# A selective-scan layer's side work re-staged: dt one tile at a time through one PSUM bank, output projections through the other

## The chip, the cores and the metric

The kernel runs on one core of one Trainium2 chip. The metric is the device time of one execution in microseconds (us), taken as the median of several runs. One execution on the chip was also taken with the hardware profiler; its trace gives the start, length and releaser of every instruction. The engines are named as in the profile: PE (TensorE, matmul), DVE (VectorE), ACT (ScalarE), POOL (GpSimd) and SP (SyncE, which only issues DMAs here).

## The reference

Four layers follow one another on a tensor of 3 x 256 x 48 x 48, each with a group norm ahead and a residual behind: an attention block, a mixture-of-experts 3x3 convolution, a plain 3x3 convolution, and a selective scan (Mamba). The change touches only the last one, except that the first two chunks of it are prepared during the third layer. All of it is float32. For each batch, with L = 2304 positions, 256 channels, 512 inner channels and 16 states:

```python
x = x + L3(_gn(x))
# L3, on tokens xf of shape (B, L, 256)
xn = (xf - mean(xf)) * rsqrt(var(xf) + 1e-5) * norm_w + norm_b
x_in, z = split(xn @ in_proj_w.T)               # 512 + 512
u  = silu(causal_conv4(x_in) + conv_b)
dt_raw, B_ssm, C_ssm = split(u @ x_proj_w.T)    # 16 + 16 + 16
dt = softplus(dt_raw @ dt_proj_w.T + dt_proj_b)
def step(h, t):
    h = h * exp(dt[t][:, None] * A) + dt[t][:, None] * B_ssm[t][None, :] * u[t][:, None]
    return h, (h * C_ssm[t][None, :]).sum(-1)
y = scan(step) + u * D_param
out = (y * silu(z)) @ out_proj_w.T
```

## The kernel before

The scan layer takes the 3 x 2304 positions in 18 chunks of 384. For each chunk the 512 inner channels are four tiles (m = 0 to 3) of 128 rows, and the 16 states of a channel are worked through in two halves (h). A pair (m, h) is a **step**, so a chunk has 8 steps, and each step has 8 **scans** (parts 0 to 7), one DVE instruction of 128 x 385 each. Four scans make a **slot**; a chunk has slots 0 to 15, and step s holds slots 2s and 2s + 1.

What belongs to the scan itself runs in a fixed pattern around each step:

- ACT computes the decay factors exp(dt * A) three scans ahead (`decay`, L1758) into three PSUM slots that rotate. So the decay for scan n + 3 can only start when scan n has ended, and DVE can go on for two more scans while ACT does something else.
- DVE scans (L1766). Between steps it fills half of the next input (`fill_upper`, L1719): three units of 768 elements ahead of an even step, one ahead of an odd step. At the end of every odd step it multiplies by the gate (`gate`, L1807).
- POOL fills the other half (L1733) and multiplies the scanned states by C (`times_c`, L1783), in turn.
- PE sums the states (`add_states`, L1795 and L1800, one PSUM bank `ps_y`) and spreads rows (`spread_pe`, L1689).

Beside it, each chunk's preparation runs one and two chunks ahead and its output projection one chunk behind. These pieces are put at slots by hand: `plan`, `after` and `gating` are lists of (slot, place, relative chunk, stage). The places within a slot are MID (after its second scan), DONE (third), LATE (fourth) and PE_ (matmuls, at LATE of an even slot and at the end of the step, ahead of `add_states`, for an odd slot). `keep_order` then ties the instructions of PE, DVE, ACT and POOL to the order in which they were written down, so each engine works strictly in that order; one that waits holds up everything behind it. SP's DMA queue works in order too.

All the side matmuls share two PSUM banks, `bank[0]` and `bank[1]`. Per chunk they pass, before the change, in this order:

- slots 0 to 4: `taps` (L1264, convolution with in_proj folded in, 8 matmuls for each tile m) for the next chunk, evacuated by `take_u` (L1273);
- slots 5 to 8: `project_y` (L1353, L1355) of the chunk before, output half 0 in bank 0 and half 1 in bank 1, evacuated by `store` (L1365);
- slot 7: `silu` of u (L1278, with a table load before and one after it, L228), then `project_u` (L1284) and `take_dbc` (L1292);
- slots 8 to 12: dt in pairs of tiles: `project_dt` (L1310) into both banks, `softplus` on ACT (L1319 to L1321: Abs, then Exp and Ln over both tiles), `take_dt` on DVE (L1326, L1327), and `keep_dt`, which copies dt out on ACT (L1331) and has SP write dt and dt*u to DRAM, from where `spread` reads them back row-replicated;
- slots 12 to 15: the token norm of the chunk after next: `group_scale` (L1213), `less_mean` (L1222, both banks), `centre` (L1235, and a square into tile `sq`, L1237), `square_mean` (L1229), `inverse_root` (L1241, L1242), `normalise` on DVE (L1246);
- slots 13 to 15: `project_z` (L1341), evacuated by `take_z` (L1349).

f32 matmuls appear as two records each in the trace.

Of the kernel before, what the change touches and what calls it, by code (L numbers as in the profile page):

```python
# [83 lines left out]
def net(  # L84
# [1041 lines left out]
    def w3_rooms():  # L1126

        block = upools[0].tile([P, 6, 3, CT, 256], F32, name="u")
        block = block.rearrange("p a b c d -> p (a b c d)")
        w3v.update(divide(  # L1130
            block, ("w3sb", P, (NW3,)), ("wtap", P, (DCONV, CT, DI * P)), ("dtsb", DTR + 1, (DI * P,)),
            ("amat", P, (DI * DS,)), ("rep", P, (4, 32)), ("less", P, (2, P)), ("zero", P, (8,)),
            ("xn0", P, (CT, CH + DCONV - 1)), ("xn1", P, (CT, CH + DCONV - 1)),
        ))
        rooms["xn"] = [w3v["xn0"], w3v["xn1"]]
        pieces = [wst.tile([P, 3 * 256], F32, name="wconv") for _ in range(6)]
        halves = [t.rearrange("p (t n) -> p t n", t=2) for t in pieces]
        for name, got in zip(("xg", "sq", "ot"), (halves[:2], halves[2:3], halves[3:5])):
            rooms[name] = got
        rooms["dbc"] = [halves[5][:96, j, :] for j in range(2)]  # L1140

# [73 lines left out]
                bias=sh[:, ct : ct + 1], scale=sc[:, ct : ct + 1],  # L1215
            )

    def less_mean(k):

        for to in range(CT):  # L1220
            for ct in range(CT):
                nc.tensor.matmul(  # L1222
                    bank[to], w3v["less"][:, int(to != ct), :], k.xg[:, ct, :],
                    start=ct == 0, stop=ct == CT - 1,
                )
# [17 lines left out]

    def normalise(k):
        rs = bank[1].unsqueeze(1).broadcast_to([P, CT, CH])
        nc.vector.tensor_tensor(k.xg, k.xg, rs, ALU.mult)  # L1246

    def tokens(k):

# [54 lines left out]
        k.dt = room(k, "dt")  # L1304
        k.dtu = room(k, "dtu")

    def project_dt(k, m0):
        for j in range(2):
            m = m0 + j
            nc.tensor.matmul(  # L1310
                bank[j], w3v["dtsb"][:, m * P : (m + 1) * P], k.dbc[: DTR + 1, :],
                start=True, stop=True,
            )

    def softplus(k, m0):

        both = k.dt[:, m0 : m0 + 2, :]
        for j in range(2):
            nc.scalar.activation(k.dt[:, m0 + j, :], bank[j], AF.Abs)  # L1319
        nc.scalar.activation(both, both, AF.Exp, scale=-1.0)  # L1320
        nc.scalar.activation(both, both, AF.Ln, bias=1.0)  # L1321

    def take_dt(k, m0):
        for j in range(2):
            m, pdt = m0 + j, bank[j]
            nc.vector.scalar_tensor_tensor(pdt, pdt, 0.0, k.dt[:, m, :], ALU.max, ALU.add)  # L1326
            nc.vector.tensor_tensor(k.dtu[:, m, :], pdt, k.u[:, m, :], ALU.mult)  # L1327

    def keep_dt(k, m0):
        for j in range(2):  # L1330
            nc.scalar.copy(k.dt[:, m0 + j, :], bank[j])  # L1331
        if m0 == 0:
            k.dtd, k.dtud = {}, {}
        d = k.dtd[m0] = dram.tile([P, 2, CH], F32, name=f"dtd{m0}")
        nc.sync.dma_start(d, k.dt[:, m0 : m0 + 2, :])
        d = k.dtud[m0] = dram.tile([P // 2, 2, CH], F32, name=f"dtud{m0}")
        nc.sync.dma_start(d, k.dtu[P // 2 :, m0 : m0 + 2, :])

    def project_z(k, m, j):
        for ct in range(CT):  # L1340
# [7 lines left out]
            k.sz = room(k, "sz")  # L1348
        nc.scalar.copy(k.sz[:, m, :], bank[j])  # L1349

    def project_y(k, mo, lo=0, hi=DI):
        if lo == 0:
            nc.tensor.matmul(bank[mo], ident, k.ot[:, mo, :], start=True, stop=False)  # L1353
        for m in range(lo, hi):
            nc.tensor.matmul(  # L1355
                bank[mo], w("out", m * 256 + mo * P, P), k.sz[:, m, :],
                start=False, stop=m == DI - 1,
            )

# [66 lines left out]
    def early_preparation():  # L1428

        while (2, 1) not in stored:  # L1430
            yield
# [4 lines left out]
        while 2 not in norm3:
            yield
        group_scale(k)
        yield
# [29 lines left out]
        k = chunks[1]  # L1469
        for stage in (group_scale, less_mean, centre, square_mean, inverse_root, normalise):  # L1470
# [12 lines left out]
        take_dbc(k)  # L1483
        yield
        for m in (0, 2):
            project_dt(k, m)
            yield
            softplus(k, m)
            yield
            take_dt(k, m)  # L1490
            yield
            keep_dt(k, m)
            yield
# [483 lines left out]
```

## Time and profile before

| what | value |
|---|---|
| median of 3 runs | 3452.24 us (3449.96 to 3456.17) |
| the profiled execution, its own time | 3452.73 us |
| span in its trace (first to last instruction) | 3451.2 us |
| PE, DVE, ACT, POOL busy, whole span | 3115.5, 2937.4, 2353.3, 1430.3 us |
| scan stage of the last layer | from 2021 us (first fill by DVE) to the end |
| one chunk there (from one `project_dt` of slot 8 to the next, 2619.29 to 2697.84) | 78.55 us |

How to read it: the engines' shares of the whole span mix four layers; only the last 1430 us matter here. In that stage the trace repeats almost exactly from chunk to chunk, so one chunk can be read for all. A timeline line gives the start in us, the length in us (for a merged run, from the first start to the last end), engine, source line, operation, output <- input with shapes, how many were merged, and in brackets the idle time of that engine just before and what ended it. A waits line gives the waiting engine and its line, what it waited for, total us, how often, and the longest. A windows line gives the length of a stretch, busy us and instruction count of PE, PEld, DVE, ACT and POOL, the clock granted to TensorE as a share of full speed, the DMA share and GB/s.

### The profile page before, as it was taken

To read this page: it belongs to the slowest core of one execution; us is meant where nothing else is said; L and a number is where in the kernel's file an instruction comes from. 1 tells how busy PE (TensorE), PEld (TensorE's weight loads), DVE (VectorE), ACT (ScalarE), POOL (GpSimd) and SP (SyncE) were. 2 spreads that over 40 slices of the span, in tenths; PEclk is the share of its full clock that TensorE was granted. 3 is DMA by queue.
4 is the path that set the end of the run, shared out by engine and by line. 5 is a ranking of instruction groups with operands and counts; after the bars stand their busy time and mean duration, and the time that the engine had idled before them with its cause. 6 is when DMAs were issued, how large, how long until landed. Compare 5 with 4: busy or idle time off the path is not lost. (4 is left out here: it accounts for less than half of the span.)

```text
span 3451.2 us, 51999 instructions
## 1 busy us (share of the span) xinstructions
PE 3115.5 (90%) x20170; PEld 1496.8 (43%) x20170; DVE 2937.4 (85%) x3306; ACT 2353.3 (68%) x3508; POOL 1430.3 (41%) x385
## 2 busy tenths in 40 slices
PE   7999999999999999879999988888888888888885
PEld 4334343443433335457677753333344443333331
DVE  4799899859899994589965379999999999999998
ACT  3788888748888884422224467777777777777774
POOL 0000000000000001110000059999999999999997
PEclk9999999999999999999999998889999999988987
DMA  4000000010000003756302134444544444544441
GB/s 178 14 8 10 8 10 8 8 42 5 11 6 8 10 8 112 240 190 222 133 22 67 46 97 115 109 105 114 120 102 115 102 109 113 119 114 107 116 111 43
DMA packets 167603, 273.95 MB, mean 79 GB/s; under 512 B 30049, under 2 KB 134561, under 8 KB 165426
## 3 DMA queue, kind: packets, MB, share of 16 engines
q1 hardware_dynamic: 154114, 250.48, 26.9%
q10 hardware_dynamic: 13232, 20.06, 1.8%
q8 instruction: 160, 2.62, 0.3%
q14 instruction: 97, 0.79, 0.1%
HBM read 223.12 MB, written 47.10 MB: 78 GB/s over the span
## 5 line engine op out<-in xcount | busy, mean ns | idle before, releaser
L641 ACT ACTIVATE pt<-ps_s 128x1024 f32<-128x1024 f32 x972 | 942.4, 1022 | 154.7 <-PE ps_s L637 142.1
L1766 DVE TENSOR_TENSOR_SCAN hs<-ps_da,hs 128x385 f32<-128x385 f32 x1152 | 1003.9, 937 | 30.7 <-ACT ps_da L1758 27.3
L856 DVE TENSOR_TENSOR part<-part,pt 128x2048 f32<-128x2048 f32 x396 | 906.7, 2290 | 41.2 <-ACT pt L641 18.4
L1758 ACT ACTIVATE ps_da<-dtr,u 128x384 f32<-128x384 f32 x1152 | 656.5, 583 | 244.1 <-DVE hs L1766 225.9
L163 POOL TENSOR_TENSOR rstd<-ve,mhalf 128x2 f32<-128x2 f32 (+1 forms) x26 | 16.4, 631 | 1475.9 <-DVE ve L161 1475.9
L637 PE MATMUL ps_s<-q,kt 32*128 32x512 f32 (+1 forms) x4320 | 576.4, 592 | 0.1
L650 PE MATMUL acc<-pt,vt 128*32 128x512 f32 (+1 forms) x4320 | 520.9, 561 | 0.2
L1783 POOL TENSOR_TENSOR hc<-hs,x 128x3072 f32<-128x3072 f32 x72 | 445.6, 6188 | 18.9 <-DVE hs L1766 16.0
L1513 PE MATMUL ps_c<-vt,u 128*128 128x288 f32 x1728 | 432.7, 411 | 20.5 <-DVE u L262 20.5
L1783 POOL TENSOR_TENSOR hc<-hs,bc 128x3072 f32<-128x3072 f32 x71 | 437.8, 6166 | 17.3 <-DVE hs L1766 15.1
L1264 PE MATMUL ps_g<-u 128*128 128x384 f32 x1152 | 388.6, 492 | 7.4 <-ACT sz L1349 3.2
L1513 PEld LDWEIGHTS ps_c<-vt,u 128*128 128x128 f32 x1728 | 330.7, 192 | 117.1 <-issue 18.8
L1264 PEld LDWEIGHTS ps_g<-u 128*128 128x128 f32 x1152 | 214.8, 190 | 180.3 <-ACT ps_da L1758 19.3
L637 PEld LDWEIGHTS ps_s<-q,kt 32*128 32x128 f32 x4320 | 195.2, 183 | 199.1 <-issue 120.2
L1800 PE MATMUL ps_y<-hc,u 128*32 128x384 f32 x2304 | 245.0, 548 | 19.6 <-POOL hc L1783 19.1
L1733 POOL TENSOR_TENSOR hs<-dtur,x 128x1536 f32<-128x1536 f32 x72 | 248.9, 3457 | 6.3 <-DMA dtur<-dtud 6.3
L1733 POOL TENSOR_TENSOR hs<-dtur,bc 128x1536 f32<-128x1536 f32 x72 | 248.5, 3451 | 0.0
L650 PEld LDWEIGHTS acc<-pt,vt 128*32 128x32 f32 x4320 | 94.4, 108 | 353.4 <-issue 326.7
L1310 PE MATMUL ps_g<-wconv,u 17*128 17x384 f32 x144 | 79.2, 684 | 85.0 <-ACT x L1331 85.0
L1800 PEld LDWEIGHTS ps_y<-hc,u 128*32 128x32 f32 x2304 | 64.2, 117 | 177.8 <-issue 143.1
L1222 PE MATMUL ps_g<-wconv,u 128*128 128x384 f32 x144 | 80.3, 725 | 62.1 <-ACT x L1331 62.1
L321 POOL MEMSET xpad<- 128x212 f32 x12 | 5.7, 472 | 313.4 <-ACT xpad L1564 234.9
(246 smaller groups left out, 3624.0 us busy)
## 6 DMA issues: line engine op xcount, KB each, us to landing
wconv<-in_we SPq DMA_DIRECT2D x144, 384.0 KB, 4.2
dtr<-dtd SPq DMA_DIRECT2D x288, 192.0 KB, 3.9
dtur<-dtud SPq DMA_DIRECT2D x288, 96.0 KB, 4.2
wconv<-xd SPq DMA_DIRECT2D x36, 384.0 KB, 4.3
x<-bcd SPq DMA_DIRECT2D x72, 192.0 KB, 6.0
dtd<-x SPq DMA_DIRECT2D x36, 384.0 KB, 3.1
bc<-bcd SPq DMA_DIRECT2D x72, 192.0 KB, 6.0
yc<-ycat ACTq DMA_DIRECT2D x18, 576.0 KB, 4.7
```

Of the source, the lines that this page charges most:

```text
L637: nc.tensor.matmul(s[:, j, cols], kt[r, mt * P : (mt + 1) * P], q[r, :n], start=True, stop=True,)
L641: nc.scalar.activation(p[:, h0 : h0 + 2, :], s, AF.Exp)
L650: nc.tensor.matmul(acc[h * HD : (h + 1) * HD, :n], vt[:, mt, g * P + h * HD : g * P + (h + 1) * HD], p[:, h, cols], start=mt == 0, stop=mt ...
L856: ): nc.vector.tensor_tensor(part, first, p, ALU.add)
L1222: nc.tensor.matmul(bank[to], w3v["less"][:, int(to != ct), :], k.xg[:, ct, :], start=ct == 0, stop=ct == CT - 1,)
L1264: nc.tensor.matmul(bank[m % 2], w3v["wtap"][:, tap, ct, m * P : (m + 1) * P], k.xn[:, ct, tap : tap + CH], start=tap == 0 and ct == 0, sto ...
L1513: nc.tensor.matmul(pc[:, :HN], u[:, i, dy, ct, m * P : (m + 1) * P], vt[:, i, ct, dy * TW : dy * TW + HN], start=ct == 0 and dy == 0, stop ...
L1733: nc.gpsimd.tensor_tensor(states(s)[:, :, 2:4, 1:], chunks[at].rows[m][1].unsqueeze(1).broadcast_to([P, 2, 2, CH]), b_rows(s, 0, 2), ALU.mult,
L1758: nc.scalar.activation(slots[n % 3][:, 1 : CH + 1], chunks[at].rows[m][0][:, q, :], AF.Exp, scale=amat[:, col : col + 1],)
L1766: nc.vector.tensor_tensor_scan(b, slots[(8 * s + part) % 3][:, : CH + 1], b, 0.0, ALU.mult, ALU.add)
L1783: nc.gpsimd.tensor_tensor(hc, tiles[s][:, :, :, 1:], cb.broadcast_to([P, 2, 4, CH]), ALU.mult)
L1800: nc.tensor.matmul(k.y_ps[32 * q : 32 * q + 32, :CH], fold, hc[:, g, q, :], start=False, stop=h == 1 and g == 1,)
```

## The change

All of dt now goes tile by tile through bank 0, `project_y` and the norm go through bank 1, and a new place BEGIN (after the first scan of a slot) is used. The plan lists, which fix the order on every engine:

```diff
-    MID, DONE, LATE, PE_ = range(4)
+    BEGIN, MID, DONE, LATE, PE_ = range(5)
     plan = [
-        (12, MID, 2, group_scale),
-        (12, PE_, 2, less_mean),
-        (13, LATE, 2, centre),
+        (11, MID, 2, group_scale),
+        (11, PE_, 2, lambda k: less_mean(k, 0)),
+        (12, DONE, 2, lambda k: centre(k, 0)),
+        (12, PE_, 2, lambda k: less_mean(k, 1)),
+        (13, LATE, 2, lambda k: centre(k, 1)),
+        (13, LATE, 2, squares),
         (13, PE_, 2, square_mean),
...
         (8, LATE, 1, take_dbc),
         (8, PE_, 1, lambda k: project_dt(k, 0)),
-        (9, LATE, 1, lambda k: softplus(k, 0)),
-        (10, MID, 1, lambda k: take_dt(k, 0)),
-        (10, DONE, 1, lambda k: keep_dt(k, 0)),
-        (10, PE_, 1, lambda k: project_dt(k, 2)),
+        (9, MID, 1, lambda k: softplus(k, 0)),
+        (9, LATE, 1, lambda k: take_dt(k, 0)),
+        (10, BEGIN, 1, lambda k: keep_dt(k, 0)),
+        (10, BEGIN, 1, lambda k: project_dt(k, 1)),
+        (10, DONE, 1, lambda k: softplus(k, 1)),
+        (11, BEGIN, 1, lambda k: take_dt(k, 1)),
+        (11, MID, 1, lambda k: keep_dt(k, 1)),
+        (11, MID, 1, lambda k: project_dt(k, 2)),
         (11, LATE, 1, lambda k: softplus(k, 2)),
-        (12, MID, 1, lambda k: take_dt(k, 2)),
-        (12, DONE, 1, lambda k: keep_dt(k, 2)),
+        (12, BEGIN, 1, lambda k: take_dt(k, 2)),
+        (12, MID, 1, lambda k: keep_dt(k, 2)),
+        (12, MID, 1, lambda k: project_dt(k, 3)),
+        (12, LATE, 1, lambda k: softplus(k, 3)),
+        (13, MID, 1, lambda k: take_dt(k, 3)),
+        (13, DONE, 1, lambda k: keep_dt(k, 3)),
     ]
     after = [
...
-        (5, PE_, -1, lambda k: project_y(k, 0)),
-        (6, LATE, -1, lambda k: store(k, 0)),
-        (6, PE_, -1, lambda k: project_y(k, 1)),
-        (8, MID, -1, lambda k: store(k, 1)),
+        (8, MID, -1, lambda k: project_y(k, 0)),
+        (9, DONE, -1, lambda k: store(k, 0)),
+        (10, MID, -1, lambda k: project_y(k, 1)),
+        (11, DONE, -1, lambda k: store(k, 1)),
     ]
```

The stages themselves, cut to what differs:

```diff
-    def less_mean(k):
-        for to in range(CT):
-            for ct in range(CT):
-                nc.tensor.matmul(bank[to], w3v["less"][:, int(to != ct), :], k.xg[:, ct, :], ...)
+    def less_mean(k, to, at=1):
+        for ct in range(CT):
+            nc.tensor.matmul(bank[at], w3v["less"][:, int(to != ct), :], k.xg[:, ct, :], ...)
-    def centre(k):
-        for ct in range(CT):
-            nc.scalar.copy(k.xg[:, ct, :], bank[ct])
-        k.sq = room(k, "sq")
-        nc.scalar.activation(k.sq, k.xg, AF.Square)
+    def centre(k, to, at=1):
+        if to == 0:
+            k.xc = room(k, "xc")
+        nc.scalar.copy(k.xc[:, to, :], bank[at])
+    def squares(k):
+        nc.scalar.activation(k.xg, k.xc, AF.Square)
-    def softplus(k, m0):
-        both = k.dt[:, m0 : m0 + 2, :]
-        for j in range(2):
-            nc.scalar.activation(k.dt[:, m0 + j, :], bank[j], AF.Abs)
-        nc.scalar.activation(both, both, AF.Exp, scale=-1.0)
-        nc.scalar.activation(both, both, AF.Ln, bias=1.0)
+    def softplus(k, m, at=0):
+        t = k.dt[:, m, :]
+        nc.scalar.activation(t, bank[at], AF.Abs)
+        nc.scalar.activation(t, t, AF.Exp, scale=-1.0)
+        nc.scalar.activation(t, t, AF.Ln, bias=1.0)
-    def keep_dt(k, m0):
-        for j in range(2):
-            nc.scalar.copy(k.dt[:, m0 + j, :], bank[j])
...
-        nc.sync.dma_start(d, k.dt[:, m0 : m0 + 2, :])
...
-        nc.sync.dma_start(d, k.dtu[P // 2 :, m0 : m0 + 2, :])
+    def keep_dt(k, m, at=0):
+        nc.scalar.copy(k.dt[:, m, :], bank[at])
...
+        nc.sync.dma_start(d, k.dt[:, m, :])
...
+        nc.sync.dma_start(d, k.dtu[P // 2 :, m, :])
```

`project_dt` and `take_dt` likewise take one tile and bank 0; `project_y` and `store` take bank 1, except at the very end of the kernel, where both banks are used as before. In `spread` the tile `dtur` loses a padding: it was [128, 2, 16 + 384] of which 384 columns from the eighth on were used, and is now [128, 2, 384]. The first two chunks, which are prepared during the third layer, go through both banks as before, in the same order and with the same number of pauses.

On PE the order of one chunk from slot 5 on was `project_y` 0, `add_states`, `spread_pe`, `project_y` 1, `project_u`, `add_states`, `project_dt` 0 and 1, `add_states`. It is now `add_states`, `spread_pe`, `project_u`, `add_states`, `project_y` 0, `project_dt` 0, `add_states`, `spread_pe`, `project_dt` 1, `project_y` 1, `project_dt` 2, `less_mean` 0, `add_states`, `project_dt` 3, `less_mean` 1, `square_mean`.

More of the change, by code (lines that the diff above doesn't have):

```diff
@@ L1137, in w3_rooms @@
         halves = [t.rearrange("p (t n) -> p t n", t=2) for t in pieces]
-        for name, got in zip(("xg", "sq", "ot"), (halves[:2], halves[2:3], halves[3:5])):
+        for name, got in zip(("xg", "xc", "ot"), (halves[:2], halves[2:3], halves[3:5])):
             rooms[name] = got
@@ L1216, in group_scale @@
             )
-    def less_mean(k):
-        for to in range(CT):
-            for ct in range(CT):
[L1222 to L1225, printed above, removed]
+    def less_mean(k, to, at=1):
+        for ct in range(CT):
+            nc.tensor.matmul(
+                bank[at], w3v["less"][:, int(to != ct), :], k.xg[:, ct, :],
+                start=ct == 0, stop=ct == CT - 1,
+            )
+    def centre(k, to, at=1):
[4 more added lines that the diff above has]
+        nc.scalar.activation(k.xg, k.xc, AF.Square)
     def square_mean(k):
@@ L1229, in square_mean @@
             nc.tensor.matmul(
-                bank[1], mean2, k.sq[:, ct, :], start=ct == 0, stop=ct == CT - 1
+                bank[1], mean2, k.xg[:, ct, :], start=ct == 0, stop=ct == CT - 1
             )
-    def centre(k):
-        for ct in range(CT):
-            nc.scalar.copy(k.xg[:, ct, :], bank[ct])
-        k.sq = room(k, "sq")
-        nc.scalar.activation(k.sq, k.xg, AF.Square)
     def inverse_root(k):
@@ L1245, in normalise @@
         rs = bank[1].unsqueeze(1).broadcast_to([P, CT, CH])
-        nc.vector.tensor_tensor(k.xg, k.xg, rs, ALU.mult)
+        nc.vector.tensor_tensor(k.xg, k.xc, rs, ALU.mult)
     def tokens(k):
@@ L1305, in take_dbc, with project_dt, take_dt @@
         k.dtu = room(k, "dtu")
-    def project_dt(k, m0):
-        for j in range(2):
[L1309 to L1313, printed above, removed]
-    def softplus(k, m0):
-        both = k.dt[:, m0 : m0 + 2, :]
-        for j in range(2):
-            nc.scalar.activation(k.dt[:, m0 + j, :], bank[j], AF.Abs)
-        nc.scalar.activation(both, both, AF.Exp, scale=-1.0)
[L1321 to L1327, printed above, removed]
-    def keep_dt(k, m0):
-        for j in range(2):
-            nc.scalar.copy(k.dt[:, m0 + j, :], bank[j])
-        if m0 == 0:
+    def project_dt(k, m, at=0):
+        nc.tensor.matmul(
+            bank[at], w3v["dtsb"][:, m * P : (m + 1) * P], k.dbc[: DTR + 1, :],
+            start=True, stop=True,
+        )
+    def softplus(k, m, at=0):
[3 more added lines that the diff above has]
+        nc.scalar.activation(t, t, AF.Ln, bias=1.0)
+    def take_dt(k, m, at=0):
+        p = bank[at]
+        nc.vector.scalar_tensor_tensor(p, p, 0.0, k.dt[:, m, :], ALU.max, ALU.add)
+        nc.vector.tensor_tensor(k.dtu[:, m, :], p, k.u[:, m, :], ALU.mult)
+    def keep_dt(k, m, at=0):
+        nc.scalar.copy(k.dt[:, m, :], bank[at])
+        if m == 0:
             k.dtd, k.dtud = {}, {}
-        d = k.dtd[m0] = dram.tile([P, 2, CH], F32, name=f"dtd{m0}")
-        nc.sync.dma_start(d, k.dt[:, m0 : m0 + 2, :])
-        d = k.dtud[m0] = dram.tile([P // 2, 2, CH], F32, name=f"dtud{m0}")
-        nc.sync.dma_start(d, k.dtu[P // 2 :, m0 : m0 + 2, :])
+        d = k.dtd[m] = dram.tile([P, CH], F32, name=f"dtd{m}")
+        nc.sync.dma_start(d, k.dt[:, m, :])
+        d = k.dtud[m] = dram.tile([P // 2, CH], F32, name=f"dtud{m}")
+        nc.sync.dma_start(d, k.dtu[P // 2 :, m, :])
     def project_z(k, m, j):
@@ L1349, in take_z, with project_y @@
         nc.scalar.copy(k.sz[:, m, :], bank[j])
-    def project_y(k, mo, lo=0, hi=DI):
+    def project_y(k, mo, lo=0, hi=DI, at=1):
         if lo == 0:
-            nc.tensor.matmul(bank[mo], ident, k.ot[:, mo, :], start=True, stop=False)
+            nc.tensor.matmul(bank[at], ident, k.ot[:, mo, :], start=True, stop=False)
         for m in range(lo, hi):
             nc.tensor.matmul(
-                bank[mo], w("out", m * 256 + mo * P, P), k.sz[:, m, :],
+                bank[at], w("out", m * 256 + mo * P, P), k.sz[:, m, :],
                 start=False, stop=m == DI - 1,
@@ L1362, in residual, with store @@
         nc.sync.dma_start(k.ot, xd[k.b][:, :, k.c * CH : (k.c + 1) * CH])
-    def store(k, mo):
-        nc.scalar.copy(k.ot[:, mo, :], bank[mo])
+    def store(k, mo, at=1):
+        nc.scalar.copy(k.ot[:, mo, :], bank[at])
         nc.sync.dma_start(
@@ L1441, in early_preparation @@
             fold_taps(winx, cwb, tap)
-        less_mean(k)
+            less_mean(k, tap, tap)
         yield
-        centre(k)
+        for ct in range(CT):
+            centre(k, ct, ct)
+        squares(k)
         yield
@@ L1469, in early_preparation @@
         k = chunks[1]
-        for stage in (group_scale, less_mean, centre, square_mean, inverse_root, normalise):
+        group_scale(k)
+        yield
+        for ct in range(CT):
+            less_mean(k, ct, ct)
+        yield
+        for ct in range(CT):
+            centre(k, ct, ct)
+        squares(k)
+        yield
+        for stage in (square_mean, inverse_root, normalise):
             stage(k)
@@ L1484, in early_preparation @@
         yield
[L1485 to L1493, printed above, removed]
+        for m0 in (0, 2):
+            for stage in (project_dt, softplus, take_dt, keep_dt):
+                for j in range(2):
+                    stage(k, m0 + j, j)
+                yield
         for m in (0, 2):
@@ L1675, in spread @@
             dtr = scn.tile([P, 4, CH], F32, name="dtr")
-            dtur = scn.tile([P, 2, 16 + CH], F32, name="dtur")[:, :, 8 : 8 + CH]
+            dtur = scn.tile([P, 2, CH], F32, name="dtur")
             for t, src in ((dtr, k.dtd), (dtur, k.dtud)):
-                src = src[m & 2][:, m & 1, :]
+                src = src[m]
                 for i in range(4):
@@ L1831, in net @@
                     first_states(s + 1)
+                if part % 4 == 0:
+                    run(at, j, BEGIN)
                 if part % 4 == 1:
@@ L1856, in net @@
         for mo in range(2):
-            project_y(k, mo, 0, DI - 1)
+            project_y(k, mo, 0, DI - 1, mo)
         add_states(end)
@@ L1860, in net @@
         for mo in range(2):
-            project_y(k, mo, DI - 1, DI)
-            store(k, mo)
+            project_y(k, mo, DI - 1, DI, mo)
+            store(k, mo, mo)
         keep_order(tc, listed, mark)
```

## The prediction

> **What bounds the kernel now.** I read in this order: busy time by stretch, the waits of DVE and POOL, then one chunk as a timeline on DVE, PE and ACT. First a stretch of the scan stage (us, then busy us of PE, PEld, DVE, ACT, POOL, granted PE clock, DMA):
>
> ```profile
> 2400.00:2600.00 200.00, 169.49 (x720) 79.19 (x712) 192.19 (x228) 155.65 (x295) 193.78 (x42) 0.91 0.47 110
> ```
>
> DVE and POOL are both nearly full, so the waits must tell which one leads. From 2100 to 3400 us:
>
> ```profile
> DVE hs L1766 <- ACT ps_da L1758: 25.7, 34, 0.9
> DVE ps_g L1326 <- ACT x L1321: 10.0, 16, 0.6
> ...
> POOL hc L1783 <- DVE hs L1766: 29.6, 18, 1.9
> ```
>
> POOL waits for DVE once per chunk; DVE waits for ACT and PE, not for POOL, until the last chunk. So DVE leads: a chunk lasts as long as DVE's work plus its waits, 78.55 us. POOL comes right behind: `times_c` starts every 9.55 us when it does not wait (2691.58, 2701.14), 8 x 9.55 = 76.4 us a chunk. Hence no edit can gain more than 2.15 us a chunk, while every us that DVE waits longer is paid in full.
>
> DVE from the end of step 3 (which I call **zero**, 2689.47 us):
>
> ```profile
> 2688.59 0.96 DVE L1766 TENSOR_TENSOR_SCAN hs<-ps_da,hs 128x385 f32<-128x385 f32 x1 [0.75 <-ACT ps_da L1758]
> 2689.47 0.53 DVE L1807 TENSOR_TENSOR x<-ps_y,x 128x384 f32<-128x384 f32 x1
> 2689.92 2.61 DVE L1719 TENSOR_TENSOR hs<-ps_r,x 128x1536 f32<-128x1536 f32 x2
> 2692.45 6.92 DVE L1766 TENSOR_TENSOR_SCAN hs<-ps_da,hs 128x385 f32<-128x385 f32 x8
> 2699.28 0.93 DVE L1719 TENSOR_TENSOR hs<-ps_r,x 128x768 f32<-128x768 f32 x1
> 2700.13 1.80 DVE L1766 TENSOR_TENSOR_SCAN hs<-ps_da,hs 128x385 f32<-128x385 f32 x2
> 2702.55 0.57 DVE L1326 SCALAR_TENSOR_TENSOR ps_g<-ps_g,x 128x384 f32<-128x384 f32 x1 [0.63 <-ACT x L1321]
> ```
>
> A scan costs 0.855 us (8 in 6.83), gate and even-step fills 2.98, the odd-step fill 0.85. PE at the same time:
>
> ```profile
> 2684.17 0.81 PE L1353 MATMUL ps_g<-wconv,ident 128*128 128x384 f32 x2
> 2684.81 2.74 PE L1355 MATMUL ps_g<-sz,u 128*128 128x384 f32 x8
> 2687.49 1.50 PE L1800 MATMUL ps_y<-hc,u 128*32 128x384 f32 x16
> ...
> 2693.09 2.76 PE L1284 MATMUL ps_g<-u 128*96 128x384 f32 x8
> 2695.68 0.81 PE L1795 MATMUL ps_y<-x,diag 128*128 128x384 f32 x2
> 2696.42 1.50 PE L1800 MATMUL ps_y<-hc,u 128*32 128x384 f32 x16
> 2697.84 1.55 PE L1310 MATMUL ps_g<-wconv,u 17*128 17x384 f32 x4
> 2699.33 1.50 PE L1800 MATMUL ps_y<-hc,u 128*32 128x384 f32 x16
> ```
>
> See that the two `project_y` (L1353, L1355) fill the time in which PE waits for `silu` of u anyway: ACT ends it at 2692.97, and `project_u` follows at 2693.09.
>
> **The change, part by part.** All times from zero, costs per chunk, with PE at full clock first.
>
> 1. *`project_y` 0 moves between `project_u` and the first `project_dt`.* PE keeps the written order, so the first dt tile now waits for: `silu` at 3.5, start of `project_u` 3.6, its 2.59 (2693.09 to 2695.68), `add_states` 2.16 (to 2697.84), `project_y` 3.32 (2684.17 to 2687.49), one `project_dt` 0.75 (half of 2697.84 to 2699.33). That is 12.4. ACT comes to `softplus` 0 at 8.8 (scan 5 of step 4 ends at 2.98 + 6 x 0.855 = 8.1, then 0.1 and a decay of 0.58) and waits 3.6 with the decays queued behind it. Three dependent ACT operations on 128x384 cost about 1.6 (0.48 for a copy or Abs; L1241 to L1242 0.59 apart), so dt is ready at 14.05. DVE arrives at `take_dt` 0 after 2.98 + 6.83 = 9.8 and waits **4.2**.
> 2. *The other three tiles.* `take_dt` 1 and 3 have only two scans (1.71) between Abs's place and DVE's arrival; ACT needs 0.1 + 0.58 + 1.6 and what it carries from `keep_dt` (0.48) and `centre`. Going through ACT's order instruction by instruction I get waits of 0.55 and 0.85; tile 2 has gate and fills (2.98) between, and about 0.1 is left. Sum **1.5**, with bounds 0 and 2.5 (three times 0.85).
> 3. *Gone:* the wait for the pair's `softplus`, **0.63**; the 0.75 on the last scan of step 3 (ACT stood 1.66 in `store` 0 for a late `project_y`), **0.75**; and of the 0.82 that DVE waits in step 7 about **0.6**, since one copy of `centre` (0.64 with its wait) leaves the chain to `square_mean`. Next late there is `square_mean` itself, some 0.2.
> 4. *At no cost:* DVE's work is the same. ACT's 8 small Exp/Ln in place of 4 larger ones add about 0.6 us busy, in the gaps of 0.27 that it has after almost each decay; without that cover it would be 0.6. The stores at slots 9 and 11 find their result ready. `keep_dt` issues 8 DMAs a chunk, not 4; tile 3's comes one slot later than before, but `spread` of it is only issued at slot 8 of the next chunk, some 11 slots of 4.9 us on; on the path, one write and read would cost the 3.1 and 3.9 us that such DMAs take to land. SP's queue already stands up to 14.1 us in one wait with nobody held up. `dtur` without padding may change POOL's fill (3.45) either way; POOL will have 2.15 us plus DVE's new waits of slack a chunk, so it can lose over 0.7 on each of 8 fills, and a gain is worth nothing.
>
> At full clock: 4.2 + 1.5 - 0.63 - 0.75 - 0.6 = **+3.7 us a chunk**.
>
> 5. *PE's clock.* Without the two `project_y`, PE comes from `taps` (to 2684.2) straight to `add_states` (1.4) and `spread_pe` (0.9) and is done at 2686.5; zero, without the wait of 0.75, lies at 2688.7. So PE stands idle from 2.2 ahead of zero to 3.6 after it, **5.8 us**. What that does is in the trace, since chunk 0 has no output projection behind it:
>
> ```profile
> 2062.59 4.96 PE L1284 MATMUL ps_g<-u 128*96 128x384 f32 x8 [7.12 <-ACT u L1278]
> ...
> 2067.59 0.58 ACT L1292 ACTIVATE wconv<-ps_g,ident 96x384 f32<-96x384 f32 x1 [1.44 <-PE ps_g L1284]
> ```
>
> `project_u` took 4.96 there, not 2.76: 2.2 more. And after the 5.05 us idle ahead of today's second `project_dt`, in every chunk:
>
> ```profile
> 2704.00:2706.00 2.00, 0.00 (x0) 0.00 (x0) 1.97 (x4) 0.33 (x1) 2.00 (x1) 0.81 1.09 215
> 2706.00:2708.00 2.00, 1.28 (x2) 0.83 (x3) 2.00 (x3) 2.00 (x6) 2.00 (x2) 0.50 1.09 215
> 2708.00:2714.00 6.00, 5.25 (x21) 1.43 (x19) 6.00 (x8) 4.71 (x11) 6.00 (x2) 0.50 0.34 107
> 2714.00:2716.00 2.00, 0.76 (x8) 0.00 (x0) 1.97 (x4) 1.74 (x4) 2.00 (x1) 0.63 0.00 0
> ```
>
> The clock falls to half at about 2705.2 and comes back at about 2715.5, ten us later. The 8.8 us of PE work of part 1 are now the path, so bounds are 0 (clock kept) and 4.0 (half speed for 8 us, as in this row). The nearest rows, 2.2 in chunk 0 and 1.8 for `less_mean` (8 records in 4.54 after 3.88 us idle, against 2.7 for 8 of 16 in 5.43), give **2.0**.
>
> [...]
>
> **The sum.** 3.7 + 2.0 = 5.7 us a chunk, for the 16 chunks (1 to 16) that have both a projection behind and a dt ahead: 91. Chunk 0 has no projection; parts 2 and 3 without the 0.75 give it about +1; chunk 17 has no dt and showed no waits that could go. The profiled execution took 3452.73 us (span 3451.2 and 1.5 around), 0.5 above the median of 3452.24, so no correction: 3452.7 + 92 = **3545 us**.
>
> **Rivals.**
> - *Clock kept, or mostly* (idle ends up shorter, or the window falls well): 16 x 3.7 + 1 = 60, 3513. For it: after 3.88 us idle the clock was only partly lost. Against: 5.05 lost it in all chunks of the stretch read. Chance 0.16.
> - *Clock lost for long*, as in the ten-us row: 16 x 7.7 + 1 = 124, 3577. Chance 0.10.
> - *`project_y` costs nothing there.* It decides whether PE delivers the first dt by 8.8 after zero; by 12.4 it is 3.6 late, about `project_y`'s own 3.32. Were it there in time, `take_dt` 0 would still wait 0.6, and 0.6 + 1.5 - 1.98 = +0.1 a chunk: 3455, no change. Chance 0.04.
> - *Faster:* the mechanism is that waits on ACT leave the leading DVE chain (part 3) and nothing replaces them, because smaller pieces fit ACT's gaps. Its place is slots 6 to 14, its price 1.98 a chunk, just under POOL's limit of 2.15: 17 x 1.98 = 34, 3419. It decides from the point where part 1 and 2 together stay under 1.98; I count 5.7 at full clock. Chance 0.06.
>
> **How the numbers follow.** Forecast 0.64, own range 3522 to 3565 (clock loss 1 to 3.2). The range 3500 to 3576 takes in the first two rivals and the bounds of part 5, and leaves out the faster and the unchanged case. About 0.2% (7 us) is what a measurement of this kernel tells from no change: faster 0.06, same 0.04, slower 0.90.
>
> **What would show it.** Right: DVE waits some 6 us once a chunk for the first tile's Ln ahead of `take_dt`; ACT's first Abs waits 3 to 6 us for PE; PE idles 5 to 6 us ahead of `project_u`, released by `silu`, at a clock near 0.5; no wait of ACT in `store`, none of DVE at the end of step 3; POOL's wait for DVE grows to 7 or more a chunk. Wrong: if `project_y` stood ahead of `project_u` on PE, if ACT found the first dt ready, or if the wait sat at tiles 1 to 3.

## The result and the profile after

| | before | after |
|---|---|---|
| median | 3453.8 us (3449.96 to 3456.17) | 3565.28 us (3561.81 to 3569.68) |
| ratio | | 1.0322, 95% interval 1.0309 to 1.0335 |
| profiled execution | 3452.73 us | 3561.81 us |
| one chunk of the scan stage (start of one `normalise` to the next, mean of 13) | 78.506 us | 85.332 us |

The change costs 111.5 us; 3545 was forecast. One chunk of the changed kernel, as DVE's timeline, the lines with a wait alone. Columns as before: start, length, instruction, idle before and what ended it. The end of step 3 (zero) is 2737.14 here:

```profile
2737.14 0.53 DVE L1821 TENSOR_TENSOR x<-ps_y,x 128x384 f32<-128x384 f32 x1
...
2746.70 0.96 DVE L1780 TENSOR_TENSOR_SCAN hs<-ps_da,hs 128x385 f32<-128x385 f32 x1 [0.53 <-ACT ps_da L1772]
2753.58 0.57 DVE L1323 SCALAR_TENSOR_TENSOR ps_g<-ps_g,x 128x384 f32<-128x384 f32 x1 [5.93 <-ACT x L1319]
...
2760.34 0.57 DVE L1323 SCALAR_TENSOR_TENSOR ps_g<-ps_g,x 128x384 f32<-128x384 f32 x1 [0.47 <-ACT x L1319]
...
2773.77 0.57 DVE L1323 SCALAR_TENSOR_TENSOR ps_g<-ps_g,x 128x384 f32<-128x384 f32 x1 [0.55 <-ACT x L1319]
...
2783.19 0.96 DVE L1780 TENSOR_TENSOR_SCAN hs<-ps_da,hs 128x385 f32<-128x385 f32 x1 [1.43 <-ACT ps_da L1772]
```

The 0.75 at the end of step 3 is gone; `take_dt` 0 (L1323) waits 5.93. The waits that the change touches sum to 0.53 + 5.93 + 0.47 + 0.55 + 1.43 = 8.91 a chunk, against 0.75 + 0.63 + 0.82 = 2.20 before: 6.7 x 16 = 107 of the 109 us between the two profiled executions. PE and ACT in the same chunk, first PE (the line at 2757.55 is `project_dt` 1, of use further below):

```profile
2740.68 4.90 PE L1285 MATMUL ps_g<-u 128*96 128x384 f32 x8 [5.55 <-ACT u L1279]
2745.41 0.81 PE L1809 MATMUL ps_y<-x,diag 128*128 128x384 f32 x2
2746.15 1.50 PE L1814 MATMUL ps_y<-hc,u 128*32 128x384 f32 x16
2747.58 0.91 PE L1349 MATMUL ps_g<-wconv,ident 128*128 128x384 f32 x2
2748.33 2.74 PE L1351 MATMUL ps_g<-sz,u 128*128 128x384 f32 x8
2751.00 0.91 PE L1309 MATMUL ps_g<-wconv,u 17*128 17x384 f32 x2
...
2757.55 0.91 PE L1309 MATMUL ps_g<-wconv,u 17*128 17x384 f32 x2 [0.89 <-ACT x L1327]
...
2778.64 2.93 PE L1236 MATMUL ps_g<-wconv,mean 128*128 128x384 f32 x4 [4.30 <-ACT wconv L1232]
```

```profile
2751.95 0.49 ACT L1317 ACTIVATE x<-ps_g 128x384 f32<-128x384 f32 x1 [4.68 <-PE ps_g L1309]
...
2781.60 0.56 ACT L1242 ACTIVATE ps_g<-ps_g,epst 128x384 f32<-128x384 f32 x1 [1.78 <-PE ps_g L1236]
```

See the chain as it was foretold: `silu` ends, `project_u` (L1285) at 4.90 in place of 2.76, `add_states`, `project_y` (L1349, L1351), the first `project_dt` (L1309), then Abs (L1317), for which ACT stood 4.68. At the end of the chunk `square_mean` (L1236) takes 2.93 after an idle 4.30, and DVE's scan ahead of `normalise` waits 1.43. Before the change these were 1.56 after 1.44, and 0.82:

```profile
2724.63 1.56 PE L1229 MATMUL ps_g<-wconv,mean 128*128 128x384 f32 x4 [1.44 <-ACT wconv L1237]
2727.81 0.96 DVE L1766 TENSOR_TENSOR_SCAN hs<-ps_da,hs 128x385 f32<-128x385 f32 x1 [0.82 <-ACT ps_da L1758]
```

POOL after the change, from 2100 to 3500 us:

```profile
POOL hc L1797 <- ACT wconv L1213: 78.4, 15, 6.8
POOL hc L1797 <- DVE hs L1780: 61.1, 33, 5.1
```

It now waits some 8.5 us a chunk (139.5 us in 16.4 chunks) for DVE's scans. The ACT instruction named in the first line is no input of `times_c`; it ends at about the time at which DVE ends the scans of step 5 (2764.21 and 2764.07 in the chunk above).

### The profile page after: what moved, and what is told of

It reads as the page before. It is cut to its first block, busy times and chain, and to the rows that moved or that the text cites. A ratio compares the mean times of both kernels' runs of the same rounds, so it can differ in the third digit from the quotient of the medians.

```text
span 3560.1 us, 52249 instructions
## 1 busy us (share of the span) xinstructions
PE 3152.0 (89%) x20170; PEld 1514.5 (43%) x20170; DVE 2939.8 (83%) x3306; ACT 2369.0 (67%) x3582; POOL 1432.4 (40%) x385
## 5 line engine op out<-in xcount | busy, mean ns | idle before, releaser
L1814 PE MATMUL ps_y<-hc,u 128*32 128x384 f32 x2304 | 226.1, 512 | 20.4 <-POOL hc L1797 19.9
L1323 DVE SCALAR_TENSOR_TENSOR ps_g<-ps_g,x 128x384 f32<-128x384 f32 x72 | 40.3, 560 | 126.3 <-ACT x L1319 126.2
L1733 DVE TENSOR_TENSOR hs<-ps_r,x 128x768 f32<-128x768 f32 (+1 forms) x108 | 127.8, 1210 | 4.4 <-DMA xd<-vt 2.2
```

Source lines behind the costliest of these rows:

```text
L1733: nc.vector.tensor_tensor(states(s)[:, lo:hi, 0:2, 1:], k.ps[:, :, :CH].unsqueeze(1).broadcast_to([P, hi - lo, 2, CH]), b_rows(s, lo, hi), ...
L1814: nc.tensor.matmul(k.y_ps[32 * q : 32 * q + 32, :CH], fold, hc[:, g, q, :], start=False, stop=h == 1 and g == 1,)
```

## The experiments

Theory 1 is the prediction's: `project_y` 0 lies on the chain silu, `project_u`, dt 0, and PE loses its clock in the idle time that it left. Theory 2: what costs is dt tile by tile through one bank, with two scans of cover for each tile, and the norm's halves. All times are medians; "chunk" is the period from one `normalise` to the next, mean of the last 13, and "steps" the same divided by 3.413 us, the step in which the granted clock switches, of which more below.

| kernel | median, us | ratio to before (95%) | chunk, us | steps |
|---|---|---|---|---|
| before | 3453.8 | | 78.506 | 23.00 |
| changed | 3565.3 | 1.0322 (1.0309 to 1.0335) | 85.332 | 25.00 |
| y0_ahead | 3509.5 | 1.0170 (1.0153 to 1.0187) | 81.940 | 24.01 |
| keep_clock | 3569.0 | 1.0341 (1.0324 to 1.0359) | 85.350 | 25.00 |
| y1_behind_alone | 3564.5 | 1.0328 (1.0311 to 1.0345) | 85.234 | 24.97 |
| no_pad | 3453.2 | 1.0005 (0.9995 to 1.0014) | 78.506 | 23.00 |
| before_more_dve | 3455.2 | 1.0002 (0.9993 to 1.0012) | 78.502 | 23.00 |
| after_more_dve | 3569.8 | 1.0331 (1.0311 to 1.0351) | 85.338 | 25.00 |
| tiles_later | 3470.4 | 1.0044 (1.0027 to 1.0061) | 79.705 | 23.35 |
| before_shifted | 3455.5 | 1.0004 (0.9994 to 1.0013) | 78.515 | 23.00 |
| before_more_dve6 | 3476.1 | 1.0059 (1.0041 to 1.0078) | 79.829 | 23.39 |
| after_more_dve6 | 3611.5 | 1.0455 (1.0436 to 1.0474) | 88.000 | 25.78 |
| y_restored | 3511.5 | 1.0167 (1.0148 to 1.0187) | 81.926 | 24.00 |
| y_restored_shifted | 3452.6 | 0.9992 (0.9983 to 1.0002) | 78.505 | 23.00 |

**y0_ahead**, the changed kernel with one line different:

```diff
-        (8, MID, -1, lambda k: project_y(k, 0)),
+        (7, PE_, -1, lambda k: project_y(k, 0)),
```

> The changed kernel with one line different: project_y 0 is put at slot 7 ahead of project_u on PE, not at slot 8 behind it; all else, dt tile by tile included, is as changed. Theory 1 (project_y 0 lies on the chain silu, project_u, dt 0, and the idle PE ahead of it loses its clock): the first take_dt's wait of 5.9 us and the 0.53 ahead of it shrink to about 1.0, as 3.3 of project_y and 2.2 of half clock leave the chain; 5.5 x 16 = 88 us less than the changed kernel's 3562 profiled, about 3473. Theory 2 (the pieces of dt with two scans of cover through one bank cost the time): dt 0 still has only two scans, so less than 1 us a chunk is gained, 3545 or more.

Measured: 56 us less than the changed kernel. One matmul group of 3.3 us ahead of another group instead of behind it, with the same work, halves the loss, so theory 2 alone does not hold. But 88 were expected. PE:

```profile
2716.12 4.51 PE L1285 MATMUL ps_g<-u 128*96 128x384 f32 x8 [2.13 <-ACT u L1279]
```

and DVE:

```profile
2725.22 0.57 DVE L1323 SCALAR_TENSOR_TENSOR ps_g<-ps_g,x 128x384 f32<-128x384 f32 x1 [2.50 <-ACT x L1319]
```

`project_y`'s part left the first wait (6.46 to 2.77 with 0.27 lost within the eight scans ahead of it), the clock's did not: after only 2.13 us of idle time `project_u` still took 4.51. And the second tile's wait doubled to 0.99: its `project_dt` now ran at half clock (1.64 in place of 0.91).

**keep_clock**: both `project_y` computed once more at their old places, those results thrown away.

```diff
+        (5, PE_, -1, lambda k: project_y(k, 0, at=0)),
+        (6, PE_, -1, lambda k: project_y(k, 1)),
         (8, MID, -1, lambda k: project_y(k, 0)),
```

> The changed kernel with both project_y computed a second time, ahead of project_u at their old places, and that result thrown away: 20 more matmul records a chunk, only to keep PE busy in the 5.6 us in which it waits for silu. Theory 1: project_u takes 2.7 again instead of 4.9, the first take_dt's waits fall from 6.5 to about 4.3, since project_y stays on the chain; 2.2 x 16 = 35 us faster than the changed kernel, about 3527. If the clock does not matter there, or PE's load is the limit: no gain, or up to 6.6 us a chunk slower (3562 to 3668).

PE, and below it DVE:

```profile
2742.55 2.74 PE L1285 MATMUL ps_g<-u 128*96 128x384 f32 x8
...
2757.26 1.64 PE L1309 MATMUL ps_g<-wconv,u 17*128 17x384 f32 x2 [0.89 <-ACT x L1327]
```

```profile
2720.23 0.56 DVE L1823 TENSOR_TENSOR sz<-ps_y,sz 128x384 f32<-128x384 f32 x1 [0.97 <-PE ps_y L1816]
...
2738.51 0.56 DVE L1823 TENSOR_TENSOR x<-ps_y,x 128x384 f32<-128x384 f32 x1 [0.36 <-PE ps_y L1816]
2739.34 2.62 DVE L1735 TENSOR_TENSOR hs<-ps_r,x 128x1536 f32<-128x1536 f32 x2 [0.27 <-PE ps_r L1705]
...
2753.30 0.57 DVE L1323 SCALAR_TENSOR_TENSOR ps_g<-ps_g,x 128x384 f32<-128x384 f32 x1 [4.52 <-ACT x L1319]
...
2760.58 0.57 DVE L1323 SCALAR_TENSOR_TENSOR ps_g<-ps_g,x 128x384 f32<-128x384 f32 x1 [0.99 <-ACT x L1319]
```

The clock's share is confirmed where it was claimed: `project_u` is back at 2.74, and the waits up to the first tile fall from 6.46 to 4.52 (4.3 expected). The time does not fall at all, against the 35 us that the expectation counted. DVE gives back 0.51 and 0.36 at the gates (0.97 and 0.36, against 0.46 and none) and 0.27 at a fill, all of them waits for PE, which has 6.6 us more work a chunk; and 0.52 at the second tile, whose `project_dt` takes 1.64 at half clock where it took 0.91. Together that is 1.66 of the 1.94 won. So a loss at one place is not a gain of the same size when it is taken away.

**y1_behind_alone**: the kernel before with `project_y` 1 behind `project_u`, and dt still in pairs.

```diff
-        (6, PE_, -1, lambda k: project_y(k, 1)),
-        (8, MID, -1, lambda k: store(k, 1)),
+        (8, MID, -1, lambda k: project_y(k, 1)),
+        (8, LATE, -1, lambda k: store(k, 1)),
```

> The kernel before with one part of the change alone: project_y 1 behind project_u (slot 8) and its store at LATE of slot 8; dt stays in pairs of tiles, the norm in both banks, project_y 0 at slot 5. Theory 1: project_y 1 (3.3) now ends 11.7 us after the end of step 3, ACT waits for it in store with the decays queued behind, and DVE loses about 4.5 a chunk at the end of step 4: 72 us, about 3525. PE idles only 3.2 us ahead of project_u, so the clock should mostly hold. Theory 2: without dt by tiles there is little to lose, at most 1 us a chunk, 3453 to 3470.

3565, as slow as the whole change. DVE loses 5.87 at the last scan of step 4, while ACT stands 6.34 in `store`:

```profile
2754.57 0.96 DVE L1766 TENSOR_TENSOR_SCAN hs<-ps_da,hs 128x385 f32<-128x385 f32 x1 [5.87 <-ACT ps_da L1758]
```

```profile
2753.11 0.48 ACT L1365 COPY wconv<-ps_g 128x384 f32<-128x384 f32 x1 [6.34 <-PE ps_g L1355]
```

So a `project_y` behind `project_u` can cost this much with dt in pairs. But the way is another than in the changed kernel: there ACT stands in Abs for dt and never in `store`. The run does not price the change's own place. The clock was not held, though PE idles the same 3.19 us in every chunk; `project_u` in three of them:

```profile
2146.39 5.43 PE L1284 MATMUL ps_g<-x,u 128*96 128x384 f32 x8 [3.19 <-ACT x L1278]
...
2488.65 2.82 PE L1284 MATMUL ps_g<-x,u 128*96 128x384 f32 x8 [3.19 <-ACT x L1278]
...
2743.21 4.37 PE L1284 MATMUL ps_g<-u 128*96 128x384 f32 x8 [3.19 <-ACT u L1278]
```

Same idle time, 2.82 to 5.43: it is not the length of the gap alone that decides. The one chunk with 2.82 lasted 83.86 us, its neighbours 85.3 to 85.4.

**no_pad**: the kernel before with `dtur` as [128, 2, 384].

> The kernel before with the padding of dtur removed and nothing else. Theory 1: POOL's fill of 3.45 us may move a little, but POOL has 2 us a chunk of slack: within 0.2% of 3453. A rival for part of the loss: the fills become slower by over 0.3 us each and POOL becomes the bound; then 144 fills x 0.1 or more, 3465 and up.

No change (ratio 1.0005): taken out alone, the padding changes nothing, and POOL's fill takes 3.4 to 3.5 us in both kernels.

**The step of the clock.** The periods of the kernels so far lie at 23, 24 and 25 times 3.413 us. The granted clock of the changed kernel, stretches of 2 us, those in which it switches (the last three numbers of a line are the clock, the DMA share and GB/s):

```profile
2738.00:2740.00 2.00, 0.00 (x0) 0.00 (x0) 2.00 (x2) 1.99 (x2) 2.00 (x1) 0.52 1.05 215
...
2744.00:2746.00 2.00, 2.00 (x6) 0.94 (x4) 2.00 (x3) 0.62 (x2) 2.00 (x1) 0.77 0.00 0
...
2758.00:2760.00 2.00, 2.00 (x5) 1.00 (x4) 1.87 (x3) 1.73 (x4) 1.20 (x1) 0.64 0.49 152
2760.00:2762.00 2.00, 2.00 (x4) 1.04 (x4) 1.62 (x3) 1.42 (x4) 0.00 (x0) 0.51 0.02 8
...
2772.00:2774.00 2.00, 2.00 (x4) 0.76 (x3) 1.45 (x3) 1.94 (x5) 1.80 (x1) 0.55 0.68 192
...
2782.00:2784.00 2.00, 2.00 (x16) 0.85 (x18) 0.81 (x1) 1.73 (x5) 2.00 (x2) 0.89 0.00 0
```

The clock records of the trace hold 1.0 and 0.5 alone, so a mean of 0.52 in 2 us puts the fall at 2738.08, and so on: falls at 2738.08, 2758.56 and 2772.20, returns at 2744.92, 2761.96 and 2782.44. The distances are 2, 4, 1, 3 and 3 times 3.41; from first to last 44.36 / 13 = 3.412. The clock records say it more sharply: from the first switch of the stage, at 2028.11, to the last, at 3557.28, are 448 steps of 3.4133, and every switch between them lies on one. So in this execution the clock switches on a grid of 3.413 us.

From this a theory of a lock: PE work that begins later within a half-clock stretch has less of it left, so lost time shrinks when work comes late and grows when it comes early, and the chunk falls in step with the grid. Then a little DVE work more should cost nothing or a whole step a chunk, never its own price.

**before_more_dve** and **after_more_dve**: in each kernel one fill of 0.855 us done twice a chunk, ahead of step 1.

```diff
-                fill_upper(s, 1, 2)
+                for _ in range(2 if m == 0 else 1):
+                    fill_upper(s, 1, 2)
```

> The kernel before with the same 0.855 us of DVE added once a chunk. Plain theory: 15 us more, 3468. Lock: its period of 78.51 us is 23 steps of 3.413, so no change (3453) or a whole step a chunk (3511), and not 3468.

> The changed kernel, with one 768-element fill of DVE (0.855 us) done twice, once in every chunk: the same values written again. Plain theory (DVE leads, every us it works more is paid): 0.855 x 18 = 15 us more, 3580. Theory of a lock (the chunk period sits on a whole number of the steps of 3.413 us in which the granted clock changes, because a later start of PE's work just means less of it at half clock): no change, 3565, or a whole step a chunk, 3.41 x 17 = 58 more.

Nothing in either: +1 and +5 us, within the spread of the runs, and the same chunk period to 0.01 us. That fits the lock, but the trace has a plainer reason. DVE at the end of step 1 in the kernel before, then in before_more_dve, there with the last scan of step 3 too:

```profile
2749.19 0.56 DVE L1807 TENSOR_TENSOR x<-ps_y,x 128x384 f32<-128x384 f32 x1 [0.40 <-PE ps_y L1800]
2750.02 2.62 DVE L1719 TENSOR_TENSOR hs<-ps_r,bc 128x1536 f32<-128x1536 f32 x2 [0.27 <-PE ps_r L1689]
```

```profile
2748.33 0.53 DVE L1808 TENSOR_TENSOR x<-ps_y,x 128x384 f32<-128x384 f32 x1
2748.78 2.61 DVE L1719 TENSOR_TENSOR hs<-ps_r,bc 128x1536 f32<-128x1536 f32 x2
...
2765.65 0.96 DVE L1767 TENSOR_TENSOR_SCAN hs<-ps_da,hs 128x385 f32<-128x385 f32 x1 [0.61 <-ACT ps_da L1759]
```

The waits of 0.40 and 0.27 for PE are gone and the 0.75 of step 3 is 0.61, so 0.81 of the 0.855 went into waits that were there already (0.82 in the changed kernel). In steps 1 to 3 it is PE, not DVE, that leads.

**before_more_dve6** and **after_more_dve6**: the same work ahead of step 6, where DVE waits for nobody.

```diff
-                fill_upper(s + 1, 0, 1)
+                for _ in range(2 if m == 3 else 1):
+                    fill_upper(s + 1, 0, 1)
```

> The kernel before with the 0.855 us fill of DVE done twice ahead of step 6 instead of step 1. Ahead of step 1 it could hide under 0.40 + 0.27 that DVE waits for PE there; between steps 5 and 7 the trace shows no wait of DVE to hide it. Plain theory: 15 us more, 3468. Lock to whole steps of 3.413 us: no change (3453) or 58 more (3511).

> The changed kernel with the 0.855 us fill of DVE done twice ahead of step 6. Plain theory: 15 us more, 3580, since DVE leads there. Lock: no change (3565) or 58 more (3623).

+22 (chunk +1.32) and +46 (chunk +2.67). The lock in its strict form falls: neither nothing nor a whole step. The plain price, 15 us, is at the very edge of the first interval and far from the second: 0.855 us of DVE work cost 2.67 a chunk there. The chunks now differ among themselves (79.12 to 80.42, and 86.30 to 88.69), where they had repeated. In after_more_dve6 the clock goes with it: in the long chunks `project_u` takes 5.25 to 5.43 and the gate of step 1 waits up to 1.34, in the short ones (86.30 to 86.36) it takes 4.41 to 4.46 and the gate waits 0.40 to 0.47. And the pattern keeps to the grid all the same: it repeats after five chunks, which take 399.36 and 440.3 us, 117 and 129 steps.

**tiles_later**, from y0_ahead (cut: tiles 1 to 3 move by one or two scans in the same way, `project_y` 1 by one):

```diff
-        (9, LATE, 1, lambda k: take_dt(k, 0)),
-        (10, BEGIN, 1, lambda k: keep_dt(k, 0)),
-        (10, BEGIN, 1, lambda k: project_dt(k, 1)),
-        (10, DONE, 1, lambda k: softplus(k, 1)),
+        (10, BEGIN, 1, lambda k: take_dt(k, 0)),
+        (10, MID, 1, lambda k: keep_dt(k, 0)),
+        (10, MID, 1, lambda k: project_dt(k, 1)),
+        (10, LATE, 1, lambda k: softplus(k, 1)),
...
-        (14, MID, 2, inverse_root),
+        (14, LATE, 2, inverse_root),
```

> The kernel y0_ahead (project_y 0 ahead of project_u) with each tile's take_dt one to two scans later, softplus 1 and 3 likewise, project_y 1 at DONE of slot 10, and inverse_root at LATE of slot 14. Plain theory: of its 5.7 us of waits a chunk (0.27, 2.50, 0.99, 0.55, 1.43) about 3.8 go: 16 x 3.8 = 61 less than 3509, about 3450. Theory 2 (dt tile by tile through one bank is what costs): the waits move but stay, above 3490. Lock: 3.41 a chunk less, 3453, or nothing.

39 of the 61 us. The waits at `take_dt` fall to 16 us in 1100 us (y0_ahead: 61 in 1380), but `normalise` then waits up to 3.1 us for `inverse_root`, which at LATE stands on ACT behind `take_z` (at DONE of slot 14) and its wait for PE's `project_z`. The chunks differ, from 78.35 to 81.83, and so does `project_u` after the same idle 2.13 us; one of a chunk of 78.44 us and one of 81.83:

```profile
2548.18 2.82 PE L1285 MATMUL ps_g<-u 128*96 128x384 f32 x8 [2.13 <-ACT u L1279]
...
2706.92 4.51 PE L1285 MATMUL ps_g<-u 128*96 128x384 f32 x8 [2.13 <-ACT u L1279]
```

PE is at half clock for 10.2 us of the first chunk and 20.5 us of the second. So within one execution, with the same work in every chunk, up to 3.4 us a chunk go with where the switches of the clock fall. With more cover, dt by tiles through one bank loses much less; y_restored_shifted below tests whether it costs anything at all.

**before_shifted**, the kernel before with

```diff
-        (6, LATE, -1, lambda k: store(k, 0)),
+        (7, MID, -1, lambda k: store(k, 0)),
-        (10, MID, 1, lambda k: take_dt(k, 0)),
-        (10, DONE, 1, lambda k: keep_dt(k, 0)),
+        (10, DONE, 1, lambda k: take_dt(k, 0)),
+        (10, LATE, 1, lambda k: keep_dt(k, 0)),
-        (14, MID, 2, inverse_root),
+        (14, LATE, 2, inverse_root),
```

> The kernel before with three places moved and nothing else: store 0 from LATE of slot 6 to MID of slot 7, take_dt and keep_dt of the first pair one scan later, inverse_root from MID to LATE of slot 14. Plain theory: DVE's waits of 0.75, 0.63 and 0.82 go, until POOL's 76.4 us a chunk bind: 17 x about 1.95 = 33 less, about 3420. Lock: no change, 3453, since 22 steps (75.1) lie under POOL's 76.4; or POOL breaks the lock and it comes out as in the plain theory.

No change. All three waits are gone, and three others stand in their place, 1.64 + 0.36 + 0.27 = 2.27 for 2.20 (the 0.40 and 0.27 at the end of step 1 are as before); DVE:

```profile
2734.23 0.95 DVE L1246 TENSOR_TENSOR wconv<-wconv,ps_g 128x768 f32<-128x768 f32 x1 [1.64 <-ACT ps_g L1242]
...
2773.05 0.56 DVE L1807 TENSOR_TENSOR sz<-ps_y,sz 128x384 f32<-128x384 f32 x1 [0.36 <-PE ps_y L1800]
2773.88 2.62 DVE L1719 TENSOR_TENSOR hs<-ps_r,bc 128x1536 f32<-128x1536 f32 x2 [0.27 <-PE ps_r L1689]
```

The largest of them is of the edit's own making: `inverse_root` now stands behind `take_z`, for which ACT waits 1.35 for PE's `project_z`:

```profile
2732.25 0.48 ACT L1349 COPY sz<-ps_g 128x384 f32<-128x384 f32 x1 [1.35 <-PE ps_g L1341]
```

So this run shows that the waits came back, but is no clean test of the lock.

**y_restored**: the changed kernel with `project_y` and `store` at their old slots and banks.

```diff
-        (8, MID, -1, lambda k: project_y(k, 0)),
-        (9, DONE, -1, lambda k: store(k, 0)),
-        (10, MID, -1, lambda k: project_y(k, 1)),
-        (11, DONE, -1, lambda k: store(k, 1)),
+        (5, PE_, -1, lambda k: project_y(k, 0, at=0)),
+        (6, LATE, -1, lambda k: store(k, 0, 0)),
+        (6, PE_, -1, lambda k: project_y(k, 1)),
+        (8, MID, -1, lambda k: store(k, 1)),
```

> The changed kernel with only project_y and store put back to the slots and banks that they had before; dt tile by tile through bank 0 and the norm in halves through bank 1 stay. Theory 1 (project_y's new place is most of the loss): plain count of waits 1.0 + 0.47 + 0.55 at take_dt, 1.43 in step 7, 0.75 at the end of step 3, 4.2 against 2.2 before: 16 x 2.0 = 32 above the kernel before, 3485; with the lock a whole number of steps: 3453 or 3507. Theory 2 (dt by tiles and the norm in halves are the loss): above 3540.

3511.5: 54 us less than the changed kernel, and 57 more than the one before. So the rest of the change (dt by tiles, the norm in halves) costs 57 us without the new place of `project_y`, and that place adds 54 to it. The waits at `take_dt` are 1.06, 0.99 and 0.77, the one of step 7 is 1.43. With 0.80 and 0.27 at the end of step 1 and 0.75 at that of step 3, DVE waits 6.07 a chunk against 2.87 in the kernel before, 3.20 of the 3.42 by which the chunk is longer. The plain count of the expectation, 4.2, left out the waits at the end of step 1 and took the second tile's 0.47 of the changed kernel; here its `project_dt` runs at half clock again (1.64 in place of 0.91).

**y_restored_shifted**: y_restored, `store` 0 at MID of slot 7, `take_dt` 0, 1 and 3 one scan later each, `inverse_root` at DONE of slot 14.

> y_restored with five places moved: store 0 to MID of slot 7, take_dt 0 to BEGIN of slot 10, take_dt 1 to MID of slot 11, take_dt 3 to DONE of slot 13, inverse_root to DONE of slot 14. A try at a kernel better than both. Plain theory: DVE's waits fall to under 1 us a chunk, 17 x about 1.5 less than before, 3427, with POOL's 76.4 us a chunk as floor (3417). Lock: 23 steps a chunk as before, 3453.

3452.6, ratio 0.9992 with an interval that holds 1: with one scan more of cover dt by tiles costs nothing against the kernel before, but does not beat it. At DONE of slot 14 `inverse_root` stands ahead of `take_z`, and `normalise` does not wait.

## Why the prediction was right, point by point

- *Part 1 and 5, the first tile:* right in mechanism and size as a wait. 4.2 + 2.0 were forecast; the trace has 6.46, of which 2.2 is `project_u` at half clock (4.90 against 2.74), and in keep_clock the wait fell by 1.94 when this clock loss was gone.
- *The split among the parts:* wrong as a price. By its own terms the new place of `project_y` was to cost 4.2 - 0.6 + 2.0 - 0.75 = 4.85 a chunk (0.6 is what the first tile would wait anyway), and all the rest 0.6 + 1.5 - 0.63 - 0.6 = 0.87. By y_restored the place is worth 3.4 a chunk (54 us) and the rest costs 3.4 (57 us). With `project_y` in time but the clock still lost, y0_ahead took 3509, where the rival of that name had 3455. So the place was priced too high and the rest far too low, and that the two errors nearly cancel in the total is luck.
- *Part 2, the other tiles:* 1.5 forecast, 0.47 + 0 + 0.55 = 1.0 measured. The second tile's 0.47 hangs on the clock: it is 0.99 where `project_dt` 1 falls into a half-clock stretch (1.64 in place of 0.91, in y0_ahead, keep_clock and y_restored).
- *Part 3, what goes:* 0.63 and 0.75 went. "Of the 0.82 that DVE waits in step 7 about 0.6" is the term that was mis-sized: it did not shrink to 0.2 but grew to 1.43, since PE idles 4.30 ahead of `square_mean` now that the halves of `less_mean` come earlier, and works at half clock afterwards (2.93 against 1.56). Where it took 2.84 (three chunks of y0_ahead, the clock falling later), the wait was 1.35. I had counted the shorter chain on ACT and not the clock a second time. 1.2 x 16 = 20 us is as much as the forecast of 3545 lacked; the first tile's 0.3 too little and the other tiles' 0.5 too much nearly cancel.
- *Part 4, no cost:* `dtur` (no_pad, in the kernel before) and the stores (no wait of ACT there) as said.
- *What bounds the kernel:* too simple. "Every us that DVE waits longer is paid in full" held for the sum of this change, but not as a rule: 15 us of DVE work more in step 1 cost nothing, in step 6 22 or 46, and the three waits taken out in before_shifted came back as others, one of them through the edit itself. In the kernel before, PE works in steps 0 to 3 without a gap from `taps` to `project_u` (2658.68 to 2695.68 in the chunk that the prediction reads), and that stretch is as tight as DVE's.
- *Rivals:* "Clock kept, or mostly" came to 3513 and failed: `project_u` took 4.89 to 5.39 in all 16 chunks, after an idle 5.55. Its "window falls well" is in the runs a matter of the clock's grid of 3.413 us: after the same idle 3.19 `project_u` took 2.82 in one chunk of y1_behind_alone and 4.32 to 5.43 in the others. "Clock lost for long" came to 3577 and lay nearer the result, 3565, than the forecast, but not by its mechanism: `project_u` lost 2.2, not 4.0. That `project_y` costs nothing there is refuted by y0_ahead, which gains 56 us from its place alone; that the kernel gets faster, by the result.
- *Two sums:* with a clock loss of 1 to 3.2 the own range would be 3529 to 3564, not 3522 to 3565, and the second rival's 3577 lies just outside the range that is said to take it in. Neither bears on the forecast. The result, 3565, stands at the upper end of the own range.

Open: why so many periods are whole numbers of the clock's step. That nine of the twelve experiments and both kernels lie on average within 0.03 of one is measured. In two of the other three the same whole number of steps returns over five chunks. That work which falls into half-clock stretches pulls the chunk there is argued; tiles_later and after_more_dve6 show chunk length and clock going together, not which drives which. A kernel whose PE never loses its clock would decide it and was not tried. So I can't say how much of y_restored's 57 us would go with its waits and how much belongs to the step to the next whole number.

## What to carry to other kernels

On an engine that keeps its order, look at what the moved work will stand behind and in front of: `project_y` filled a time in which PE waited anyway, and behind that wait the same 3.3 us cost the whole chain. A gap that is left behind on PE can be paid a second time at half clock, by the first work after it (`project_u` 4.90 after an idle 5.55, against 2.76); whether it is depends here on where the clock's switch falls (2.82 in one chunk of y1_behind_alone and 4.32 to 5.43 in the others, all after an idle 3.19). Where several engines form a ring, price a change by the run, for a wait removed at one place may come back at another, and a sum of waits can be right while the price of each part is not.

## What the runs showed of the hardware

- The granted clock switches between 1.0 and 0.5 on a grid of 3.413 us (448 steps from 2028.11 to 3557.28 in the changed kernel), and the same group of 8 matmul records took 2.82, 4.37 or 5.43 after the same idle 3.19 us (y1_behind_alone).
- An idle time of 2.13 us went with a lost clock in 15 of 16 chunks of y0_ahead (`project_u` 4.51), but in tiles_later `project_u` kept 2.82 after the same 2.13 us in 9 of 16 chunks.
- Of the two kernels and twelve experiments, eleven have a mean chunk of 23, 24 or 25 steps of that grid (within 0.03); before_more_dve6 and after_more_dve6 repeat after 117 and 129 steps for five chunks.
